# The last image's output products placed ahead of its attention sums, and the range check among the last results

## The chip, the cores and the metric

The kernel runs on one core of one Trainium2 chip. The metric is the device time of one execution in microseconds; the median of three runs before the change is 3424.28 us (3424.08 to 3426.5).

## What is computed

The reference has two layers on eight images of 64 x 64 positions with 256 channels. Layer 0 projects to q and k (v is k), does softmax attention in horizontal windows with half of the channels and in vertical windows with the other half, adds a depthwise 3 x 3 convolution of a hard-swish of v, takes a hard-swish of the sum (the context) and projects it with `w_out`. Layer 1 is attention over all 4096 positions of an image with 32-wide f, g and h, and a residual:

```
s    = g @ f^T ;  beta = softmax(s)
v    = beta @ h
out  = gamma * (v @ kv + bv) + x        # x = context @ w_out + b_out
```

So every output element is a product of the context with `w_out` plus a product of the attention's result with `wv` (scaled by gamma and a spectral norm) plus a bias. The two products are added in PSUM, the accumulator memory of TensorE.

## The kernel before, in words

Everything is float32, with channels on the 128 partitions and positions along the free axis, in blocks of TB = 512 positions. An image is a row of units: eight horizontal windows (h), eight vertical ones (v), and two global units (l), each of which handles half of the image's query positions (four blocks, one per quarter of 32 partitions) against all keys in 32 steps.

A step c of a global unit is: `scores` (four matmuls into two of three PSUM pairs s_0, s_1, s_2, L860), two exponentials on ACT (`weights_of`, L477), `weighted` (four matmuls into num_l, L876), and `add` on DVE (acc_l, L887), which sums the exponentials of all steps. The weighted product of a step is issued one step late (`flow.held`). When a unit's steps are over, these follow:

- `release` (L891) copies num_l to nums_l in SBUF on ACT.
- `sums` (L896) sums acc_l over partitions with four matmuls against ones; `copy_sums` (L497) copies the result to SBUF on ACT.
- `norm` (L902 on) takes the reciprocals on DVE (transpose L487, reciprocal L489, transpose L490) and multiplies nums_l with them (L904). In an image's second global unit it also calls `note` (L530), which keeps a running maximum and minimum of all reciprocals in the two tiles `seen`.
- `result(m, r)` makes the output: for output half m, r = 0 first issues four wv products (L915), one for each of the unit's four blocks, into two PSUM pairs with `start=True`; then, for two blocks at a time, 16 w_out products (`product`, L262) are added; then ACT adds the bias into an `ot` tile (L925) and SP issues its transfer to `out` (L926). There are two `ot` buffers (`out_bufs`).

The order of all engines' work is planned while the program is built. `Flow` keeps tasks in lanes with due times and estimated costs, and `flow.step` picks from them around each unit's scores; `flow.require(task)` issues a task and what it needs at once; `flow.drain` issues what is left. `result` tasks sit in the lane `res` and need `u.normed`. For all units but the last, there are score steps of the following unit to put around these tasks. For the last unit of the last image there is none: its sums, norm and results are issued by `flow.drain`, one behind the other.

PSUM is full with three s pairs (two banks each), num, and one bank (`mm_tile`) shared by all other products, the sums among them.

Behind the last image, the range check decides whether the fast way without subtracted maxima was valid. On DVE it takes the maximum and minimum of `seen` into `lim` (L1269, L1270), compares them with two limits (L1271, L1272), adds up the verdicts of all partitions with one matmul into `good` (L1274), and makes a flag (L1276, L1278). `nc.values_load` (L1279) loads the flag into a register of every engine, SP also asserts its bounds, and each engine branches (L1280) over an exact second pass, which does not run with these inputs. The tiles of the check come from a pool that is opened only then.

Of the kernel before, what the change touches and what calls it, by code (L numbers as in the profile page):

```python
# [5 lines left out]

# [6 lines left out]
F32 = mybir.dt.float32  # L13
I32 = mybir.dt.int32
AF = mybir.ActivationFunctionType
ALU = mybir.AluOpType
AX = mybir.AxisListType

P = 128
# [3 lines left out]
TB = 512  # L23
NB = N // TB
D = 32
NQ = P // D
L2_EPS = 1e-12

SUM_MAX, SUM_MIN = 1e20, 1e-20


def quad(r):
    return slice(r * D, (r + 1) * D)
# [225 lines left out]
def product(nc, out, lhsT, rhs, start=True, stop=True):  # L259

    for r in range(lhsT.shape[1] // D):
        nc.tensor.matmul(out[quad(r), :], lhsT=lhsT[:, quad(r)], rhs=rhs, start=start, stop=stop)  # L262
# [3 lines left out]
def tile_attention_blocks(  # L266
# [18 lines left out]
    nc = tc.nc  # L285
# [6 lines left out]
    def mm_tile(name):  # L292
        return ps_mm.tile([P, TB], F32, tag="mm", name=name)
# [4 lines left out]
    ones = const.tile([P, P], F32, name="ones")  # L298
# [29 lines left out]
    wout_sb = const.tile([P, 2, C], F32, name="wout_sb")  # L328
# [14 lines left out]
    wv_sb = const.tile([P, C], F32, name="wv_sb")  # L343
    bias_o = const.tile([P, 2], F32, name="bias_o")
# [58 lines left out]
    seen = [const.tile([P, 2 * NB + 2, TB // D], F32, name=f"seen{i}") for i in range(2)]  # L403
    for t in seen:
        nc.gpsimd.memset(t, 1.0)

    def attention(images, load_x, out_rows, exact):


# [2 lines left out]
        out_bufs = 1 if exact else 2  # L412
        state = pools.enter_context(tc.tile_pool(name=f"state{sfx}", bufs=1))
        xpool = pools.enter_context(tc.tile_pool(name=f"xpool{sfx}", bufs=2))
        work = pools.enter_context(tc.tile_pool(name=f"work{sfx}", bufs=2))
# [4 lines left out]
        ps_sc = pools.enter_context(tc.tile_pool(name=f"ps_sc{sfx}", bufs=1, space=PSUM))  # L420
# [7 lines left out]
        h_sb = state.tile([P, N // P, D], F32, name="h_sb")  # L428


        pairs = cycle([ps_sc.tile([P, 2, TB], F32, name=f"s_{i}") for i in range(3)])

        def combined_weights():

# [31 lines left out]
            return act[i // 2][:, k, start + cols.start : start + cols.stop]  # L466

        def sc_tiles():
            return [next(pairs), next(pairs)]

        def row_of(sc, r):
            return sc[r // 2][:, r % 2, :]
# [46 lines left out]
        def image(b):  # L519
# [311 lines left out]
            def global_unit(z):  # L831
                nm = f"{b}_l{z}"
                u = {}
# [74 lines left out]
                def result(m, r):  # L908
# [14 lines left out]
                    for q, j, po in blocks:  # L923
                        ot = work.tile([P, TB], F32, tag="ot", name=f"ot_{nm}_{q}_{m}", bufs=out_bufs)
                        nc.scalar.activation(ot, po, AF.Identity, bias=bias_o[:, m : m + 1])  # L925
                        nc.sync.dma_start(out=out_rows(b, m)[:, j * TB : (j + 1) * TB], in_=ot)  # L926

                return SimpleNamespace(
                    steps=4 * NB, scores=scores, weighted=weighted, add=add,
                    release=release, sums=sums, norm=norm, result=result,  # L930
                )

            return SimpleNamespace(
# [2 lines left out]
                project_fg=project_fg, fetch_fg=fetch_fg, project_h=project_h, turn_h=turn_h,  # L936
                h=[window_unit(0, i) for i in range(NB)],
                v=[window_unit(1, i) for i in range(NB)], l=[global_unit(z) for z in range(2)],
            )

        flow = Flow()
# [8 lines left out]
        units, t = [], 0  # L950
# [27 lines left out]
        def in_turn(tag, task):  # L978

            task.after += last_users[tag][-1:]  # L980

        def weights_ready(t):
            task = Task([])
            task.done, task.step = True, t
            weights[t] = task
            return task

        weights = {}
        for u in units:
            if not u.kind:  # L990
                continue
            e = u.t + u.steps
            w = [weights_ready(u.t + c) for c in range(u.steps)]
            if u.kind == "l":
                chain = None
                for c in range(1, u.steps):
                    task = flow.add(
                        "dve", [(partial(u.add, c), [("dve", ADD)])], u.t + c + DUE["add"],
                        [w[c]] + ([w[0]] if c == 1 else [chain]), ready=u.t + c + 1,
                    )  # L1000
                    if c == 1:
                        in_turn("acc", task)
                        readers[u.t].append(task)
                    readers[u.t + c].append(task)
                    chain = task
                total = flow.add(
                    "pe", [(u.sums, [("pe", PROD), ("act", COPY)])], e + 1, [chain], ready=e, bank=True
                )
                in_turn("sum", total)
                last_users["acc"].append(total)  # L1010
            else:
                acc = flow.add(
                    "dve", [(partial(u.add, 1), [("dve", ADD)])], u.t + 2, w[:2], ready=u.t + 2
                )
                in_turn("acc", acc)
                terms, pair = 3, acc
                if DUE["adds_v" if u.kind == "v" else "adds_h"]:
                    terms, acc = 2, flow.add(
                        "dve", [(partial(u.add, 2), [("dve", ADD)])], u.t + DUE["add2"],
                        [acc, w[2]], ready=u.t + 3,  # L1020
                    )
                pieces = [(partial(u.sums, n), [("pe", PROD / HALVES)]) for n in range(terms * HALVES)]
                pieces[-1] = (pieces[-1][0], [("pe", PROD / HALVES), ("act", COPY)])
                total = flow.add("pe", pieces, e, [acc, *w[2:]], ready=e, bank=True)
                total.then = (terms - 1, e + DUE["sums"])
                in_turn("sum", total)
                last_users["acc"].append(total)
                for c, task in enumerate(
                    (pair, pair, (total, 2) if terms == 3 else acc, (total, 1))
                ):  # L1030
                    readers[u.t + c].append(task)
            u.released = flow.add("act", [(u.release, [("act", COPY)])], e + DUE["release"], ready=e)
            shuffle = [("sp", ISSUE), ("dma", VIA)] if u.kind == "v" else []
            u.normed = flow.add(
                "dve", [(u.norm, [("dve", NORM), *shuffle])], e + DUE["norm"], [total, u.released], ready=e
            )
            last_users["sum"].append(u.normed)
            u.fetched = u.normed
            if u.kind == "v":
                u.fetched = flow.add("sp", [(u.fetch, [("sp", 4 * ISSUE), ("dma", FETCH)])], e, [u.normed])  # L1040
# [32 lines left out]
        for n, im in enumerate(ims):  # L1073
# [4 lines left out]
            for i in range(NB):  # L1078
                u = h[i]
# [4 lines left out]
                start = last.l[0].t if last else 0  # L1084
# [26 lines left out]
                for half in range(2):  # L1111
# [14 lines left out]
                    if p >= 0:  # L1126
                        k = 2 * p
# [58 lines left out]
            for z, u in enumerate(l):  # L1186
                u.ends = []
                for m in range(2):
                    pieces = [
                        (  # L1190
                            partial(u.result, m, r),
                            [("pe", 4 * PROD + (SCORES + DRAIN if r == 0 else 0)), ("act", 2 * EVICT)],
                        )
                        for r in (0, 2)
                    ]
                    u.ends.append(flow.add("res", pieces, u.t + u.steps + 4 * m, [u.normed], im.ends[-1:]))
                    im.ends.append(u.ends[-1])
                for r in range(NQ):
                    im.results[z * NQ + r] = u.ends
# [13 lines left out]
        for k, u in enumerate(units):  # L1213
            if u.kind:
                tag = ("ctxh", CTX) if u.kind == "h" else ("nums", 2)
# [32 lines left out]
        with tc.manual_schedule():  # L1248
            last = None
            for u in units:  # L1250
                for c in range(u.steps):
                    flow.step(partial(unit_scores, u, c), partial(unit_values, u, c, last))
                last = u
            flow.drain()
        pools.close()

    xv = xT.rearrange("b (k p) n -> b p k n", p=P)
    ov = out.rearrange("(b m p) n -> b m p n", m=2, p=P)
    attention(
        range(B),  # L1260
        lambda b, i: xv[b, :, :, i * TB : (i + 1) * TB],
        lambda b, m: ov[b, m],
        exact=False,
    )


    check = ctx.enter_context(tc.tile_pool(name="check", bufs=1))
    lim = check.tile([P, 2], F32, name="lim")
    nc.vector.tensor_reduce(lim[:, 0:1], seen[0], AX.XY, ALU.max)  # L1269
    nc.vector.tensor_reduce(lim[:, 1:2], seen[1], AX.XY, ALU.min)  # L1270
    nc.vector.tensor_single_scalar(lim[:, 0:1], lim[:, 0:1], SUM_MAX, ALU.is_le)  # L1271
    nc.vector.tensor_single_scalar(lim[:, 1:2], lim[:, 1:2], SUM_MIN, ALU.is_ge)  # L1272
    good = mm_tile("good")
    nc.tensor.matmul(good[0:1, 0:2], lhsT=ones[:, 0:1], rhs=lim, start=True, stop=True)  # L1274
    total = check.tile([1, 1], F32, name="total")
    nc.vector.tensor_reduce(total, good[0:1, 0:2], AX.X, ALU.add)  # L1276
    flag = check.tile([1, 1], I32, name="flag")
    nc.vector.tensor_copy(flag, total)  # L1278
    fine = nc.values_load(flag[0:1, 0:1], min_val=0, max_val=2 * P)  # L1279
    with tc.If(fine < 2 * P):  # L1280
        with tc.For_i(0, B) as b:
# [6 lines left out]
                exact=True,  # L1288
# [46 lines left out]
```

## Time and profile before

| | us |
|---|---|
| median of three runs | 3424.28 |
| the profiled execution's own time | 3424.36 |
| its span, first to last instruction | 3422.6 |
| PE (TensorE) busy in the span | 3334.3 |
| DVE (VectorE) busy | 2860.2 |
| ACT (ScalarE) busy | 2665.0 |
| last add of acc_l ends | 3389.26 |
| last w_out product ends | 3412.83 |
| flag written | 3414.55 |

Times in the trace are counted from the span's start. PEld is TensorE's weight load, which overlaps its matmuls. A float32 matmul of the program stands as two rows in the trace, so a block of 16 w_out products shows as x32. SPq, ACTq and so on are an engine's sequencer, which issues transfers, waits on semaphores and branches; these do not count as busy time. PEclk is the share of its full clock that TensorE was granted.

### The profile page before, as it was taken

The numbers are of one execution on the slowest core, as the hardware profiler recorded it, in microseconds if no ns is written. First come the engines' busy times: TensorE is split into PE (matmuls) and PEld (weight loads), VectorE is DVE, ScalarE is ACT, GpSimd is POOL, SyncE is SP. The second block draws the span as 40 slices with busy tenths as digits, with TensorE's granted clock in tenths as the row PEclk, the third lists the DMA queues.
The fourth block names the chain that finished last, engine by engine and source line by source line (L and its number), as shares of the span: only waits on it lengthen the run. The fifth ranks groups of instructions, "written<-read, shape, count | busy, mean of one in ns | idle before, by whom it ended". The sixth has DMA issues, their size and how long they took to land.

```text
span 3422.6 us, 78296 instructions
## 1 busy us (share of the span) xinstructions
PE 3334.3 (97%) x33780; PEld 1126.0 (33%) x33780; DVE 2860.2 (84%) x2340; ACT 2665.0 (78%) x3235; POOL 63.5 (2%) x266
## 2 busy tenths in 40 slices
PE   7989999999999999999999999999999999999997
PEld 3323333333333333333333333333333333333322
DVE  4778789887898879988799887998879988898876
ACT  5777787887878877788787887788877888778875
POOL 0000000000000000000000000000000000000000
PEclk9999999999999999999999999999999999999999
DMA  2122102221032210332112311123111231122200
GB/s 71 51 78 70 46 26 91 79 74 44 20 99 84 61 57 25 92 88 59 44 44 78 96 45 50 50 72 97 50 38 57 78 88 47 38 69 62 78 29 27
DMA packets 249411, 209.84 MB, mean 61 GB/s; under 512 B 26080, under 2 KB 190432, under 8 KB 249056
## 3 DMA queue, kind: packets, MB, share of 16 engines
q1 hardware_dynamic: 246816, 204.18, 20.2%
q8 instruction: 268, 4.39, 0.5%
q10 hardware_dynamic: 2240, 0.56, 0.1%
q14 instruction: 87, 0.71, 0.1%
HBM read 99.78 MB, written 83.89 MB: 54 GB/s over the span
## 4 chain that ended last, share of the span: by engine, by line
PE 70%; DVE 15%; ACT 8%; issue 4%; DMA 2%; SPq 1%; DVEq 0%; ACTq 0%
PE s L679 12%; DVE acc_l L887 11%; PE pq L262 11%; PE s L860 10%; PE num_l L876 9%; PE num_h L696 7%; PE s L262 6%; PE sum_h L714 5%; PE num_v L696 4%; ACT p_v L477 4%; PE sum_v L714 3%; DVE act L622 2%; PE pf L783 2%; ACT p_h L477 1%; PE s L915 1%
## 5 line engine op out<-in xcount | busy, mean ns | idle before, releaser
L887 DVE TENSOR_TENSOR acc_l<-acc_l,p_l 128x2048 f32<-128x2048 f32 x480 | 1099.6, 2291 | 224.3 <-ACT p_l L477 197.7
L477 ACT ACTIVATE p_l<-s 128x1024 f32<-128x1024 f32 x1024 | 991.4, 1023 | 188.4 <-PE s L860 121.6
L622 DVE SCALAR_TENSOR_TENSOR act<-hv,dw_sb,act 128x1024 f32<-128x1024 f32 x512 | 655.1, 1281 | 16.6 <-ACT act L618 2.3
L860 PE MATMUL s<-gq,f 32*128 32x512 f32 x4096 | 630.4, 640 | 3.8 <-ACT p_l L477 1.7
L477 ACT ACTIVATE p_h<-s 128x1024 f32<-128x1024 f32 x512 | 494.0, 1025 | 91.9 <-PE s L679 59.3
L477 ACT ACTIVATE p_v<-s 128x1024 f32<-128x1024 f32 x512 | 496.6, 1027 | 77.0 <-PE s L679 65.0
L876 PE MATMUL num_l<-p_l,h_sb 128*32 128x512 f32 x4096 | 546.4, 605 | 0.8 <-ACT nums_l L891 0.5
L262 PE MATMUL pq<-x,wqkv_sb 128*32 128x256 f32 x8192 | 520.5, 382 | 4.3 <-ACT qv L554 1.6
L262 PEld LDWEIGHTS pq<-x,wqkv_sb 128*32 128x32 f32 x8192 | 263.1, 110 | 361.4 <-issue 197.6
L679 PE MATMUL s<-qh,kh 32*128 32x512 f32 x2048 | 319.7, 640 | 11.4 <-ACT qh L551 6.6
L679 PE MATMUL s<-qv,kv 32*128 32x512 f32 x2048 | 327.3, 644 | 2.4 <-ACT p_v L477 2.4
L696 PE MATMUL num_v<-p_v,vs 128*32 128x512 f32 x2048 | 274.9, 609 | 21.2 <-DMA vs<-kvia 12.8
L860 PEld LDWEIGHTS s<-gq,f 32*128 32x128 f32 x4096 | 191.9, 183 | 311.8 <-issue 286.3
L696 PE MATMUL num_h<-p_h,vs 128*32 128x512 f32 x2048 | 272.8, 605 | 8.0 <-DMA vs<-kvia 3.3
L262 PE MATMUL s<-act,wout_sb 128*32 128x512 f32 x2048 | 227.4, 596 | 0.0
L925 ACT ACTIVATE ot_l<-s,bias_o 128x512 f32<-128x512 f32 x128 | 81.2, 684 | 179.8 <-PE s L262 168.5
L705 DVE TENSOR_TENSOR acc_v<-p_v,p_v 128x2048 f32<-128x2048 f32 x64 | 146.7, 2292 | 87.1 <-issue 60.5
L876 PEld LDWEIGHTS num_l<-p_l,h_sb 128*32 128x32 f32 x4096 | 80.7, 108 | 385.5 <-issue 370.7
L705 DVE TENSOR_TENSOR acc_h<-p_h,p_h 128x2048 f32<-128x2048 f32 x64 | 146.4, 2287 | 33.2 <-PE sum_v L714 15.6
L679 PEld LDWEIGHTS s<-qv,kv 32*128 32x128 f32 x2048 | 106.8, 184 | 181.3 <-issue 172.1
L679 PEld LDWEIGHTS s<-qh,kh 32*128 32x128 f32 x2048 | 94.0, 183 | 180.8 <-issue 140.3
L705 DVE TENSOR_TENSOR acc_v<-acc_v,p_v 128x2048 f32<-128x2048 f32 x64 | 146.2, 2284 | 4.8 <-ACT p_v L477 4.8
(126 smaller groups left out, 2464.4 us busy)
## 6 DMA issues: line engine op xcount, KB each, us to landing
x<-in_xT SPq DMA_DIRECT2D x92, 512.0 KB, 3.8
kvia<-kt SPq DMA_DIRECT2D x128, 256.0 KB, 2.5
vs<-kvia SPq DMA_DIRECT2D x512, 64.0 KB, 2.1
out<-ot_l SPq DMA_DIRECT2D x128, 256.0 KB, 2.1
via_v<-nums_v SPq DMA_DIRECT2D x64, 256.0 KB, 2.0
shuf_v<-via_v SPq DMA_DIRECT2D x256, 64.0 KB, 2.1
f<-fg SPq DMA_DIRECT2D x256, 64.0 KB, 2.0
gq<-fg SPq DMA_DIRECT2D x64, 64.0 KB, 2.0
```

Of the source, the lines that this page charges most:

```text
L262: nc.tensor.matmul(out[quad(r), :], lhsT=lhsT[:, quad(r)], rhs=rhs, start=start, stop=stop)
L477: nc.scalar.activation(pt[:, 2 * z : 2 * z + 2, :], sc[z], AF.Exp, scale=scale)
L622: nc.vector.scalar_tensor_tensor(o, src, wt, o, ALU.mult, ALU.add)
L679: nc.tensor.matmul(row_of(sc, r), lhsT=k[quad(r), c * P : (c + 1) * P], rhs=q[quad(r), :], start=True, stop=not exact,)
L696: nc.tensor.matmul(u["num"][quad(r), :], lhsT=vs[kind, i][:, r, c, :], rhs=u[c][:, r, :], start=(c == 0), stop=(c == 3),)
L705: nc.vector.tensor_add(u["acc"], u["acc"] if c == 2 else u[0], u[c])
L714: nc.tensor.matmul(u["sum"][quad(r), cols], lhsT=ones[:, :D], rhs=pt[:, r, cols], start=(k == 0), stop=(k == len(of) - 1),)
L783: nc.tensor.matmul(pf[quad(r), cols], lhsT=wcomb[:, k, quad(r % 2)], rhs=act_of(2 * p + r // 2, k, cols), start=(k == 0), stop=(k == 1),)
L860: nc.tensor.matmul(row_of(sc, r), lhsT=f4[quad(r), c * P : (c + 1) * P], rhs=gq[quad(r), z, :], start=True, stop=not exact,)
L876: nc.tensor.matmul(u["num"][quad(r), :], lhsT=h_sb[:, c, :], rhs=u[c][:, r, :], start=(c == 0), stop=(c == 4 * NB - 1),)
L887: nc.vector.tensor_add(u["acc"], u["acc"], u[c])
L925: nc.scalar.activation(ot, po, AF.Identity, bias=bias_o[:, m : m + 1])
```

## The change

For the last global unit of the last image in the fast pass, no `result` tasks are made. Two new functions issue its output in another order, written out by hand: `last_blocks(m, js)` issues the w_out products of output half m for two blocks into one PSUM pair (with `start` at the first and no stop), and `last_ends(m, js)` adds the wv products to them (`start=False, stop=True`) and issues the bias and the transfer. The PSUM pairs become a `deque`, so that one can be taken at a time.

The order at the end is now: w_out products of half 0, blocks 0 and 1; the last weighted product; w_out of half 0, blocks 2 and 3; sums and release; w_out of half 1, blocks 0 and 1; norm; wv and results of half 0; the range check's operations; wv and results of half 1, blocks 0 and 1; then w_out, wv and results of half 1, blocks 2 and 3.

The range check's pool is opened before the attention's, and its operations become the function `limits`, called between the results of half 0 and half 1. Loading the flag and the branch stay where they were in the source. In the built program, each engine's load of the flag is still the last thing before its branch, except on SP, where it stands behind the second of the last eight result transfers.

```diff
+    def limits():
+        nc.vector.tensor_reduce(lim[:, 0:1], seen[0], AX.XY, ALU.max)
+        nc.vector.tensor_reduce(lim[:, 1:2], seen[1], AX.XY, ALU.min)
+        nc.vector.tensor_single_scalar(lim[:, 0:1], lim[:, 0:1], SUM_MAX, ALU.is_le)
+        nc.vector.tensor_single_scalar(lim[:, 1:2], lim[:, 1:2], SUM_MIN, ALU.is_ge)
+        good = mm_tile("good")
+        nc.tensor.matmul(good[0:1, 0:2], lhsT=ones[:, 0:1], rhs=lim, start=True, stop=True)
+        nc.vector.tensor_reduce(total, good[0:1, 0:2], AX.X, ALU.add)
+        nc.vector.tensor_copy(flag, total)
...
+                def last_blocks(m, js):
+                    rows = slice(m * P, (m + 1) * P)
+                    if js[0] == 0:
+                        u["po", m] = []
+                    pair = pairs.popleft()
+                    pairs.append(pair)
+                    for i, j in enumerate(js):
+                        u["po", m].append(pair[:, i, :])
+                        for k in range(2):
+                            product(
+                                nc, u["po", m][j], wout_sb[:, k, rows], act_of(z * NQ + j, k),
+                                k == 0, False,
+                            )
+
+                def last_ends(m, js):
+                    rows = slice(m * P, (m + 1) * P)
+                    for j in js:
+                        nc.tensor.matmul(
+                            u["po", m][j], lhsT=wv_sb[quad(j), rows], rhs=u["num_sb"][quad(j), :],
+                            start=False, stop=True,
+                        )
+                    for j in js:
+                        ot = work.tile([P, TB], F32, tag="ot", name=f"ot_{nm}_{j}_{m}", bufs=out_bufs)
+                        nc.scalar.activation(
+                            ot, u["po", m][j], AF.Identity, bias=bias_o[:, m : m + 1]
+                        )
+                        i = z * NQ + j
+                        nc.sync.dma_start(out=out_rows(b, m)[:, i * TB : (i + 1) * TB], in_=ot)
...
+                    if u is units[-1] and not exact:
+                        continue
                     u.ends.append(flow.add("res", pieces, u.t + u.steps + 4 * m, [u.normed], im.ends[-1:]))
...
+            if not exact:
+                u.last_blocks(0, (0, 1))
+                flow.held()
+                flow.held = None
+                flow.t += 1
+                u.last_blocks(0, (2, 3))
+                flow.require(u.total, u.released)
+                u.last_blocks(1, (0, 1))
+                flow.require(u.normed)
+                u.last_ends(0, range(NQ))
+                limits()
+                u.last_ends(1, (0, 1))
+                u.last_blocks(1, (2, 3))
+                u.last_ends(1, (2, 3))
             flow.drain()
```

More of the change, by code (lines that the diff above doesn't have):

```diff
@@ L2 @@
 from contextlib import ExitStack
-from itertools import cycle
 from functools import cache, partial
@@ L405, in tile_attention_blocks @@
         nc.gpsimd.memset(t, 1.0)
+    check = ctx.enter_context(tc.tile_pool(name="check", bufs=1))
+    lim = check.tile([P, 2], F32, name="lim")
+    total = check.tile([1, 1], F32, name="total")
+    flag = check.tile([1, 1], I32, name="flag")
+    def limits():
[7 more added lines that the diff above has]
+        nc.vector.tensor_copy(flag, total)
     def attention(images, load_x, out_rows, exact):
@@ L428, in attention @@
         h_sb = state.tile([P, N // P, D], F32, name="h_sb")
-        pairs = cycle([ps_sc.tile([P, 2, TB], F32, name=f"s_{i}") for i in range(3)])
+        pairs = deque(ps_sc.tile([P, 2, TB], F32, name=f"s_{i}") for i in range(3))
         def combined_weights():
@@ L468, in sc_tiles @@
         def sc_tiles():
-            return [next(pairs), next(pairs)]
+            taken = [pairs.popleft(), pairs.popleft()]
+            pairs.extend(taken)
+            return taken
         def row_of(sc, r):
@@ L930, in global_unit @@
                     release=release, sums=sums, norm=norm, result=result,
+                    last_blocks=last_blocks, last_ends=last_ends,
                 )
@@ L1033, in attention @@
             shuffle = [("sp", ISSUE), ("dma", VIA)] if u.kind == "v" else []
+            u.total = total
             u.normed = flow.add(
@@ L1264, in tile_attention_blocks @@
     )
[L1267 to L1278, printed above, removed]
     fine = nc.values_load(flag[0:1, 0:1], min_val=0, max_val=2 * P)
```

## The prediction

> **What bounds the kernel now.** I read the page first, then the chain of waits, the timeline and the clock of the last 40 us, because the change touches only what follows the last image's last score step.
>
> ```profile
> span 3422.6 us, 78296 instructions
> PE 3334.3 (97%) x33780; PEld 1126.0 (33%) x33780; DVE 2860.2 (84%) x2340; ACT 2665.0 (78%) x3235; POOL 63.5 (2%) x266
> ```
>
> PE carries the kernel as a whole, but the tail is a different stage. The chain of waits (start, length, what), cut to its last part:
>
> ```profile
> 3386.96 2.30 DVE acc_l L887
> ...
> 3389.40 1.97 PE sum_l L896 x8
> 3391.39 0.59 ACT sum_sb_l L497
> ...
> 3394.53 2.09 PE s L915 x8
> 3396.62 8.09 PE s L262 x64
> 3404.71 1.07 PE s L915 x8
> 3405.78 7.05 PE s L262 x64
> 3412.85 0.45 DVE lim L1269
> ...
> 3414.41 0.14 DVE flag L1278
> ```
>
> The sums wait for DVE's last add (3389.26), the wv products wait for the norm (3394.49), and only then 15.1 us of w_out products start, which need neither. PE idles 4.2 us and 3.2 us on the way. The windows view gives the granted clock behind the DVE, ACT and POOL columns:
>
> ```profile
> 3383.00:3388.50 5.50, 1.97 (x8) 0.29 (x8) 5.29 (x3) 1.68 (x3) 0.00 (x0) 1.00 0.01 1
> 3388.50:3398.80 10.30, 6.20 (x28) 1.34 (x32) 3.85 (x7) 0.58 (x1) 0.00 (x0) 0.50 0.01 2
> ```
>
> After the idle stretch the clock is half for 10 us; that is why the sums take 1.97 us where num_l, four matmuls of the same shape, takes 1.07. What comes behind the flag the chain does not show; the views of L1279 and L1280, and SP's waits, do:
>
> ```profile
> L1279 SPq TENSOR_LOAD <-flag x1: 750/750/750, 3415.0 to 3415.0; - x1
> L1279 SPq SEQ_ASSERT  x1: 33/33/33, 3416.3 to 3416.3; - x1
> L1280 SPq COMPARE_BRANCH x1: 50/50/50, 3416.4 to 3416.4; - x1
> SPq L1280 <- SPq L1280: 4.2, 1, 4.2
> ```
>
> SP loads the flag, asserts its bounds, branches over the exact pass at 3416.4, and then stands 4.2 us before the next instruction. From there 1.9 us of semaphores and drains lead to 3422.6. So the end is: last result, flag, load, branch, fixed tail.
>
> **What the Trainium skill says.** "TensorE: Matmul & The Clock Gate", Part 1: an idle window of about 3.4 us drops the array to half rate until a busy one has passed. The trace agrees: 1.00, then 0.50 from 3388.5 to 3398.8. "DMA: Bandwidth & Descriptors", Anatomy of one DMA: about 2 us of fixed completion time per transfer; here 2.0 us at least and 2.1 in the middle for a 256 KB result. "Runtime: NRT & Kernel Launch", Instruction fetch mechanics: a taken branch outside the prefetched pages stalls on a fetch; the 4.2 us fit that, though only the stall, not its cause, is in the trace.
>
> **The change part by part.** The instruction order of the built program is unchanged on every queue up to the last score step. Behind it nothing is added: the same 64 w_out, 8 wv, 4 sum and 1 check matmul of the tail and the same eight result transfers, in another order. I replay that order with this trace's durations. A block of 16 w_out matmuls is half of a warm L262 row: 7.05/2 = 3.53 us.
>
> *PE.* num_l of step 30 ends at 3382.96. Block m0/q01 to 3386.49; num_l of step 31 (+1.07) to 3387.56; block m0/q23 to 3391.09. The banks are free: the exponentials that read them ended by 3384.1. The sums now start at 3391.09 instead of 3389.40, so they are 1.7 us late, but PE has not idled, so I take the warm 1.07: 3392.16, 0.8 us later than before. Block m1/q01 runs to 3395.69.
>
> *Norm.* From the sums' end to the product's end it took 3394.49 - 3391.37 = 3.12 us; now 3395.28. The nums copy, now behind the sums' copy on ACT (0.58 us), lies beside DVE's two transposes and reciprocal (1.7 us): nothing. PE is still on m1/q01, so the norm is hidden, and wv for m0 (1.07 warm) ends at 3396.76, its first half at 3396.23.
>
> *Range check.* The two seen updates end 0.74 after the norm, 3396.02; the four lim operations took 1.02 (3397.04). The good matmul, in PE's queue behind wv m0, waits some 0.4 us for lim, ends near 3397.4; the flag is ready at 3397.7. The 1.7 us of check work after the last w_out (3412.83 to 3414.55) leave the end.
>
> *PE's rest.* wv m1/q01 (0.53) to 3397.9, block m1/q23 to 3401.5, its wv to 3402.0. Before, PE ended at 3412.83: 10.8 us earlier. But PE then no longer sets the end.
>
> *ACT and the result buffers.* There are two ot buffers. Each result must have landed before its buffer is written again; before, PE gave pairs only every 3.4 to 4.6 us, which hid this. Where it shows today, in ACT's timeline of the image's first half and in the view of the ot_l tile:
>
> ```profile
> 3329.47 0.69 ACT L925 ACTIVATE ot_l<-s,bias_o 128x512 f32<-128x512 f32 x1 [2.22 <-PE s L262]
> 3331.35 0.69 ACT L925 ACTIVATE ot_l<-s,bias_o 128x512 f32<-128x512 f32 x1 [1.19 <-DMA out<-ot_l]
> DMA to landing us min/median/max: 2.0/2.1/4.4
> ```
>
> A buffer's round is 0.71 (ACT start to SP issue: 3401.36 to 3402.07) + 2.1 + 0.08 = 2.9 us. The first pair starts at 3396.30; three rounds later, 3405.0, starts the last pair (1.27 us for two): 3406.27 against 3414.17 before. PE's last block is ready at 3402.0, 3 us ahead.
>
> *SP.* Its flag load now sits between the second and third result transfer, with six transfers queued behind it. SP is free at 3397.9; semaphores 0.42, then 1.35 from load to assert: 3399.8, just when the third result (3399.2 + 0.7) is ready. I charge 0.1 us. Behind the last transfer (3406.3 + 0.33) only the branch is left: 3406.7 against 3416.44, **9.7 us earlier**. The 4.2 us fetch I keep; with the other engines branching at other times it may be 3.4 (ACT's, 3415.66 to 3419.07) or, beside two transfers in flight, up to 1.4 longer (estimate: those transfers' own time). The last landing, 3408.4, is under it. ACT, last of the other engines, loads its own flag after the last result (0.82), branches near 3407.2 and is back by 3410.6, just ahead of SP's 3410.9.
>
> Sum: 7.9 us from the results, 1.9 from check and load leaving the end, less 0.1. The profiled execution took 3424.36 (span 3422.6 and 1.8 around it), 0.1 above the median of 3424.28. Forecast: 3424.3 - 9.7 = **3414.6 us**.
>
> **The rivals.**
> *Longer rounds or fetch.* One transfer at 4.0 us, as at 3327.3 (issue to landing), adds 1.9; a fetch slowed by the last transfers adds 1.4. For it: ACT waited for a landing four times, 11.3 us in all, earlier in this run. Against: at the tail no loads share the queues, and its eight landings took 2.0 to 2.3. Gain 6.4 to 8.3: 3416 to 3418.
> *The clock falls anyway.* If PE is at half rate from 3388.55 to 3398.79 as now: block m0/q23 ends at 3393.6, sums 3395.6, m1/q01 3400.7, first pair 5 us later. Gain 4.7: 3419.6. Against: the longest gap that I find is 0.4 us.
> *Not as written.* A scheduler could hold the w_out blocks behind the norm, and the gain would be the check's 1.9 us alone: 3422.4. The built order speaks against it.
> *Slower than before.* The check's tiles are now allocated ahead of the attention's pools, so every later on-chip tile sits at a shifted address. If this slows the 480 acc_l adds (1099.6 us busy, 11% of the chain, 376 us), the gain is cancelled at 9.7/376 = 2.6% on each (2291 to 2350 ns); at 5% the kernel ends 9 us slower: 3433. Nothing shows that addresses matter here, and shapes are the same.
>
> **How the numbers follow.** A measurement of this kernel can tell about 0.2%, 6.8 us, so faster means below 3417.4. Forecast as worked out, 3412.5 to 3416: 0.74. Longer rounds or fetch: 0.15, of which 0.03 fall above 3417.4. Half clock: 0.05, within 0.2%. Not as written: 0.02, within. Slower: 0.04. That is 0.86 faster, 0.10 the same, 0.04 slower. The range starts where fetch (-0.8) and rounds (3 x -0.1) are best and the runs' spread of 2.4 us is taken by half, 3412.2, and ends with the longer rounds, 3418.3.
>
> **What would show it.** In the profile after: the clock 1.00 through 3383 to 3402; sums at 1.07 us; no PE gap over 1 us before wv; ACT's ot rows paced 2.9 us with DMA as releaser; the flag cast near 3397.7; SP's branch near 3406.7 and its stall of 4.2; the adds still 2291 ns. A half clock, a third transfer issued well after 3399.9, rounds above 3.3 us, a stall over 6 us, or longer adds would each prove its step wrong.

## The result, and the profile after

The changed kernel takes 3417.38 us in the median (3415.27 to 3420.03, 11 runs) against 3424.55 (3422.58 to 3426.85, 11 runs): 7.2 us less, ratio 0.9979 with a 95% interval of 0.997 to 0.9988. Measured once more, the same two kernels gave 3417.62 and 3424.8, ratio 0.9976 (0.9968 to 0.9984). Both intervals leave out no change; the size is just beyond the 0.2% that the prediction took as the least that can be told here. The profiled execution took 3416.28, so the two profiled executions are 8.1 us apart. From here on every time is from the profile that the text names.

The page's head, and the windows view over the new tail (columns as before; the clock is the third number from the end):

```profile
span 3414.5 us, 78286 instructions
PE 3331.6 (98%) x33780; PEld 1126.4 (33%) x33780; DVE 2860.6 (84%) x2340; ACT 2668.8 (78%) x3235; POOL 63.5 (2%) x266
```

```profile
3383.00:3402.60 19.60, 19.09 (x166) 5.46 (x158) 10.55 (x15) 5.36 (x9) 0.00 (x0) 1.00 0.15 56
```

PE is busy for 19.1 of 19.6 us at the full clock, where before it idled for 7.4 us in two gaps and had the half clock for 10 us. The chain of waits, last part:

```profile
3383.16 3.43 PE s L261 x32
...
3390.89 0.86 PE sum_l L913 x8
3391.75 3.43 PE s L261 x32
3395.18 1.08 PE s L963 x8
...
3396.29 0.70 ACT ot_l L969
...
3397.00 2.04 DMA out<-ot_l
...
3400.50 3.70 DMA out<-ot_l
...
3404.28 0.70 ACT ot_l L969
...
3404.99 2.60 DMA out<-ot_l
...
3407.67 0.69 ACT ot_l L969
```

The wait for DVE's last add, the norm and the range check have left the chain; the sums stand in it only as work of PE between two blocks. In their place stand three landings of result transfers, each followed by the ACT instruction that had to wait for its buffer. ACT's timeline says the same, with the releaser at the end of each row:

```profile
3396.29 1.27 ACT L969 ACTIVATE ot_l<-s,bias_o 128x512 f32<-128x512 f32 x2 [3.39 <-PE s L963]
3399.14 1.33 ACT L969 ACTIVATE ot_l<-s,bias_o 128x512 f32<-128x512 f32 x2 [1.59 <-DMA out<-ot_l]
3402.22 0.69 ACT L969 ACTIVATE ot_l<-s,bias_o 128x512 f32<-128x512 f32 x1 [1.75 <-DMA out<-ot_l]
3404.28 1.46 ACT L969 ACTIVATE ot_l<-s,bias_o 128x512 f32<-128x512 f32 x2 [1.37 <-DMA out<-ot_l]
3407.67 0.69 ACT L969 ACTIVATE ot_l<-s,bias_o 128x512 f32<-128x512 f32 x1 [1.94 <-DMA out<-ot_l]
```

The first round is 2.85 us (3396.29 to 3399.14), forecast 2.9; the two that start next take 3.1 and 4.5 (3399.14 to 3402.22, 3399.78 to 3404.28). The last result ends at 3408.36, forecast 3406.27. The views of the flag, of the branch line and of SP's waits complete the end:

```profile
L420 DVE CAST flag<-total x1: 141/141/141, 3397.2 to 3397.2; 1x1 int32<-1x1 f32 x1
```

```profile
L1334 POOLq COMPARE_BRANCH  x1: 45/45/45, 3398.3 to 3398.3; - x1
L1334 DVEq COMPARE_BRANCH  x1: 72/72/72, 3398.5 to 3398.5; - x1
L1334 PEldq COMPARE_BRANCH  x1: 4032/4032/4032, 3400.1 to 3400.1; - x1
L1334 SPq COMPARE_BRANCH  x1: 50/50/50, 3409.1 to 3409.1; - x1
```

```profile
SPq L1334 <- SPq L1334: 3.5, 1, 3.5
```

Two things are new here. SP branches at 3409.1, 7.4 us earlier than before, and its stall is 3.5 instead of 4.2. And DVE and PE load the early flag and branch at 3398.5 and 3400.1, in the middle of the result transfers. DVE's work is over by then; PE's sequencer branches while PE's last matmuls run on to 3402.6. POOL branches at 3398.3. In the DMA view of 3400.5 to 3404.2, the stretch of the transfer that took 3.70 us to land, queues 8 and 14 carry instructions:

```profile
q1 hardware_dynamic: 369, 0.69, 49.7%
q8 instruction: 1, 0.02, 1.5%
q14 instruction: 1, 0.01, 0.9%
```

That suggested theory A: the rounds of the two result buffers set the end, and the instruction fetches of engines that now branch early lengthen the landings in these rounds. Rival B: the landings are slow of themselves, two transfers at a time. Rival C: something else sets the end, PE's rest or SP's flag load.

### The profile page after: what moved, and what is told of

Read it like the earlier page. It is cut to its first block, busy times and chain, and to the rows that moved or that the text cites. A ratio compares the mean times of both kernels' runs of the same rounds, so it can differ in the third digit from the quotient of the medians.

```text
span 3414.5 us, 78286 instructions
## 1 busy us (share of the span) xinstructions
PE 3331.6 (98%) x33780; PEld 1126.4 (33%) x33780; DVE 2860.6 (84%) x2340; ACT 2668.8 (78%) x3235; POOL 63.5 (2%) x266
## 4 chain that ended last, share of the span: by engine, by line
PE 71%; DVE 14%; ACT 8%; issue 4%; DMA 2%; SPq 1%; DVEq 0%; ACTq 0%
PE s L696 12%; PE s L877 11%; PE pq L261 11%; DVE acc_l L904 10%; PE num_l L893 10%; PE num_h L713 7%; PE s L261 6%; PE sum_h L731 5%; PE num_v L713 4%; ACT p_v L494 4%; PE sum_v L731 3%; DVE act L639 2%; PE pf L800 2%; ACT p_h L494 1%; PE s L932 1%
## 5 line engine op out<-in xcount | busy, mean ns | idle before, releaser
L904 DVE TENSOR_TENSOR acc_l<-acc_l,p_l 128x2048 f32<-128x2048 f32 x480 | 1099.8, 2291 | 224.5 <-ACT p_l L494 197.9
```

The costliest lines, as they stand in the source:

```text
L904: nc.vector.tensor_add(u["acc"], u["acc"], u[c])
```

## The experiments

All edits are against the changed kernel unless the text says otherwise. Each ratio is to the kernel before on the same chip; the first four shared one chip (before: 3423.15 us), the last three another (3424.8 us). Each experiment has one profile. The place in the span where the tail begins varies from profile to profile by some us (DVE's last add ends between 3385.6 and 3389.8), so I compare stretches inside the tail: from the start of the first result on ACT to the end of the last.

### Eight result buffers

```diff
-ot = work.tile([P, TB], F32, tag="ot", name=f"ot_{nm}_{j}_{m}", bufs=out_bufs)
+ot = work.tile([P, TB], F32, tag=("qh", "kh")[m], name=f"ot_{nm}_{j}_{m}", bufs=QH)
```

> The changed kernel, with the last unit's eight results in eight buffers of their own (the idle ones of qh and kh) instead of two in turn. Theory A (rounds of the two result buffers set the end, and their landings are lengthened by instruction fetches of engines that branch early): ACT no longer waits for a landing, the last result follows PE's last product (3402.6) and ends near 3403.9 instead of 3408.4, SP branches near 3404.4 instead of 3409.1; 4 to 5 us faster than the changed kernel, 11 to 13 us faster than before. Rival B (rounds set the end, but slow landings come from the transfers themselves, which stand two at a time): the same here, landings above 2.3 stay. Rival C (PE's rest or SP's flag load sets the end): no change, 0 to 1 us.

Measured: 3411.35 us, ratio 0.9968 (0.9956 to 0.998), 11.8 us under before. ACT's timeline:

```profile
3394.30 3.58 ACT L969 ACTIVATE ot_l<-s,bias_o 128x512 f32<-128x512 f32 x6 [3.40 <-PE s L963]
3400.70 1.26 ACT L969 ACTIVATE ot_l<-s,bias_o 128x512 f32<-128x512 f32 x2 [2.82 <-PE s L963]
```

No row waits for a DMA any more. Six results run back to back, the last two follow PE, and first to last takes 7.66 us (3394.30 to 3401.96) against 12.07 in the changed kernel: 4.4 us less. SP branches at 3402.7. So the buffers' rounds did set the end, and rival C falls. The landings themselves became longer (up to 3.6 us, with up to four transfers in flight and instruction packets beside the longest; this run does not separate the two), which no longer matters. Theory A and rival B both expected this result; the next experiment tells them apart.

### The branches of DVE and PE held back

```diff
+hold = check.tile([P, 2], F32, name="hold")
+nc.vector.tensor_copy(hold, u.last_ot[:, 0:2])
+held = mm_tile("held")
+nc.tensor.matmul(held[0:1, 0:2], lhsT=ones[:, 0:1], rhs=hold, start=True, stop=True)
```

Here `u.last_ot` is the buffer of the last result.

> The changed kernel, with one small DVE copy out of the last result and one small matmul of it added behind everything, so that DVE and PE branch after the last result, while the flag stays early for SP. Theory A (fetches of early branches lengthen the landings): all landings that ACT waits for are 2.0 to 2.3 us, the last result ends near 3406.3 instead of 3408.4; the end itself gains less, 0 to 2 us, since PE and DVE then fetch last. Rival B (landings are slow of themselves): landings of 2.3 to 3.7 us again, last result near 3408, and the kernel slower than the changed one by 0 to 1 us.

Measured: 3414.88 us, ratio 0.9975 (0.9965 to 0.9984), 8.3 us under before. ACT's timeline:

```profile
3395.72 1.27 ACT L970 ACTIVATE ot_l<-s,bias_o 128x512 f32<-128x512 f32 x2 [3.40 <-PE s L964]
3398.57 1.33 ACT L970 ACTIVATE ot_l<-s,bias_o 128x512 f32<-128x512 f32 x2 [1.58 <-DMA out<-ot_l]
3401.42 1.33 ACT L970 ACTIVATE ot_l<-s,bias_o 128x512 f32<-128x512 f32 x2 [1.53 <-DMA out<-ot_l]
3404.27 1.33 ACT L970 ACTIVATE ot_l<-s,bias_o 128x512 f32<-128x512 f32 x2 [1.51 <-DMA out<-ot_l]
```

The rows start 2.85 us apart, every time. The six landings that are waited for took 2.02 to 2.11 us, and first to last is 9.88 us; the prediction's sum gave 9.97 for this stretch. In the DMA view of the same stretch as above (from the issue of the fourth transfer, 3.7 us long) no instruction packet starts:

```profile
q1 hardware_dynamic: 406, 0.77, 54.8%
```

Nothing about these transfers was changed, only when DVE and PE branch. So rival B falls: the 2.2 us of excess in the changed kernel come with the early branches of DVE and PE. That the branches act through their fetches is read from the packets (see the last section). POOL still branches early here, and one 8 KB instruction packet starts at 3399.22, beside a landing of 2.04, which it did not lengthen. The end itself gains less: from the first result to the span's end it is 16.4 us, against 18.2 and 17.7 in the two profiles of the changed kernel (the second is below), because PE is now the last to come back:

```profile
L1342 POOLq COMPARE_BRANCH  x1: 45/45/45, 3397.7 to 3397.7; - x1
L1342 SPq COMPARE_BRANCH  x1: 50/50/50, 3406.3 to 3406.3; - x1
L1342 PEldq COMPARE_BRANCH  x1: 3662/3662/3662, 3407.3 to 3407.3; - x1
```

Whether it beats the changed kernel the intervals can't tell.

### The range check late

```diff
-                limits()
...
+    limits()
     fine = nc.values_load(flag[0:1, 0:1], min_val=0, max_val=2 * P)
```

> The changed kernel, with the range check's operations called behind the last results, as before, but with its tiles still allocated first. DVE and PE then load the flag and branch only after PE's last product, near 3403 to 3404, not near 3398 and 3400. Theory A: the landings of the first two pairs of results go back to 2.0 to 2.3 us, the last result ends near 3406.3 to 3407.0; SP's flag load is in time for the last pair, so the kernel is 1 to 2 us faster than the changed one. Rival B: landings and time as in the changed kernel, or up to 1.5 us slower for the later flag.

Measured: 3414.56 us, ratio 0.9973 (0.9962 to 0.9983), 8.6 us under before. The branches of DVE and PE, and ACT's timeline:

```profile
L1334 PEldq COMPARE_BRANCH  x1: 4212/4212/4212, 3402.3 to 3402.3; - x1
L1334 DVEq COMPARE_BRANCH  x1: 72/72/72, 3402.6 to 3402.6; - x1
```

```profile
3394.99 1.26 ACT L969 ACTIVATE ot_l<-s,bias_o 128x512 f32<-128x512 f32 x2 [3.40 <-PE s L963]
3397.84 1.32 ACT L969 ACTIVATE ot_l<-s,bias_o 128x512 f32<-128x512 f32 x2 [1.58 <-DMA out<-ot_l]
3400.72 1.31 ACT L969 ACTIVATE ot_l<-s,bias_o 128x512 f32<-128x512 f32 x2 [1.55 <-DMA out<-ot_l]
3403.56 0.69 ACT L969 ACTIVATE ot_l<-s,bias_o 128x512 f32<-128x512 f32 x1 [1.54 <-DMA out<-ot_l]
3404.78 0.69 ACT L969 ACTIVATE ot_l<-s,bias_o 128x512 f32<-128x512 f32 x1 [0.53 <-DMA out<-ot_l]
```

DVE and PE branch at 3402.6 and 3402.3, 7.6 and 7.3 us after the first result's start (in the changed kernel 2.2 and 3.8). The first four landings took 2.03 to 2.11 us; of the two that the last pair waits for, one took 2.65. First to last is 10.48 us: between the other two, as theory A says. SP's flag load fits ahead of the last pair and costs nothing. SP's stall was 4.4 us, though, so from the first result to the span's end it is 17.6 us, against 18.2 and 17.7 in the two profiles of the changed kernel. The 1 to 2 us expected over the changed kernel can't be told. So for this order the late check is no worse than the early one, as far as the intervals show: the order of the w_out products gives the gain without the check's move.

### Only the check moved early, order of before

The kernel before, with the check's pool opened first and `limits` called after the results of half 0; no `last_blocks`, no `last_ends`:

```diff
                         nc.sync.dma_start(out=out_rows(b, m)[:, j * TB : (j + 1) * TB], in_=ot)
+                    if not exact and b == B - 1 and z and (m, r) == (0, 2):
+                        limits()
```

> The kernel before, with only the range check moved: its operations between the results of half 0 and half 1, its tiles allocated first. The w_out and wv order is that of before. By the prediction's steps: the last result ends as before (3414.2), and the 1.9 us of check, flag load and assert leave the end: SP branches near 3414.6 instead of 3416.4, 1.6 to 2.6 us faster than before (the upper end if SP's fetch is as short as in the changed kernel, 3.5 instead of 4.2). If the check was hidden anyway: 0.

Measured: 3422.06 us, ratio 0.9996 (0.9988 to 1.0004): 1.1 us under before, less than the 1.6 to 2.6 expected. The interval neither tells it from no change nor rules the expectation out (0.9988 is 4.1 us). The step itself is there: from the last result's end to SP's branch it was 2.27 us (3414.17 to 3416.44) and is 0.70 (3415.15 to 3415.84), 1.6 us less. Part of it goes to PE's clock in the profile. The half-clock stretch lies 1.9 us later here. That shortens the sums by 0.5 us (1.45 against 1.94), and the 64 rows of half 0's w_out products that meet it take 0.95 us longer:

```profile
3396.56 9.11 PE L261 MATMUL s<-act,wout_sb 128*32 128x512 f32 x64
3405.49 0.19 PE L418 MATMUL good<-lim,ones 128*1 128x2 f32 x2
```

The same row before:

```profile
3396.55 8.16 PE L262 MATMUL s<-act,wout_sb 128*32 128x512 f32 x64
```

SP's stall is 0.5 us shorter (3.7 against 4.2), and from DVE's last add to the span's end it is 31.8 us against 33.3. So the check's move is worth about 1.6 us in the order of before, where PE sets the end. In the new order, where the result buffers set it, the late check showed no loss against the early one. The larger part of the gain is the order of w_out.

### The changed kernel again

> The changed kernel once more, as it is, on the chip of the two runs that follow. Theory A (landings lengthened where an instruction fetch is in flight, by branches that come early): among the landings that ACT waits for, those with a fetch beside them are above 2.2 us, those without are 2.0 to 2.2; the last result ends 10 us after the first one starts plus the excess of these landings over 2.1; 6 to 9 us faster than before. Rival B (slow landings of themselves): long landings without a fetch beside them.

Measured: 3417.62 us, ratio 0.9976 (0.9968 to 0.9984). First to last 11.69 us. The six landings waited for: 2.03, 2.12, 2.40, 3.69, 2.00 and 2.24. The DMA view shows one packet on each instruction queue beside the 3.69 again, and one on q8 beside the 2.00, so a fetch in flight does not always lengthen a landing, which I had expected of it; but of these six none above 2.2 stands without one.

### The first two blocks behind the sums

```diff
-                u.last_blocks(0, (0, 1))
                 flow.held()
                 flow.held = None
                 flow.t += 1
-                u.last_blocks(0, (2, 3))
                 flow.require(u.total, u.released)
+                u.last_blocks(0, (0, 1))
+                u.last_blocks(0, (2, 3))
                 u.last_blocks(1, (0, 1))
```

> The changed kernel, with its first two blocks of w_out products put behind the sums instead of ahead of and between the last weighted product and the sums; all else as changed. By the prediction's clock step, PE idles again from 3385 to 3389.4, and the half clock comes back for about 7 to 10 us: sums in 1.5 to 2 us, first results near 3405 instead of 3396.3, last result near 3415 to 3417, no faster than before: -1 to +2 us. If the clock played no part and only the order counted: the three blocks (10.6 us) from 3390.5, first results near 3402, last near 3412, 3 to 5 us faster than before.

Measured: 3423.04 us, ratio 0.9997 (0.9988 to 1.0005): the whole gain is gone. PE's timeline and the windows view:

```profile
3385.94 1.91 PE L913 MATMUL sum_l<-acc_l,ones 128*32 128x512 f32 x8 [4.20 <-DVE acc_l L904]
3387.54 11.46 PE L261 MATMUL s<-act,wout_sb 128*32 128x512 f32 x96
```

```profile
3386.00:3389.50 3.50, 3.50 (x20) 1.18 (x24) 0.96 (x2) 1.07 (x2) 0.00 (x0) 0.51 0.02 5
3389.50:3402.00 12.50, 12.32 (x113) 4.13 (x107) 3.34 (x11) 1.27 (x2) 0.00 (x0) 1.00 0.03 10
```

The 4.2 us gap is back, and with it the half clock, but for 3.4 us only, not for the 7 to 10 that I expected. In the kernel before it lasted 10.2 us, and there PE idled again behind the sums, while here it had work without a gap; that this made the difference is argued from the two traces, not tested. At full rate these 3.4 us of work take half, 1.7 us. From the end of DVE's last add to the first result it is 14.3 us (3385.79 to 3400.11); in the changed kernel 6.8 (3389.46 to 3396.29), 7.5 less. The two blocks that now stand behind the sums are 6.9 of it (3.43 each), the clock 1.7, less 1.1 by which the sums here start sooner after the add. So most of the gain is cover, not clock: 5.8 us net from work put into time in which PE would wait for DVE, and about 1.7 us of clock on top in this profile.

### Eight buffers, and the last bias on DVE

On top of the eight buffers:

```diff
+if (m, j) == (1, NQ - 1):
+    nc.vector.tensor_scalar_add(ot, u["po", m][j], bias_o[:, m : m + 1])
+else:
     nc.scalar.activation(ot, u["po", m][j], AF.Identity, bias=bias_o[:, m : m + 1])
```

> The eight buffers of the first experiment, and the very last result's bias added by DVE beside ACT instead of behind it. Theory A: as the eight buffers, with the last result 0.5 us earlier: 11 to 13 us faster than before; the DVE now branches behind it, so that fewer fetches fall beside the transfers. Rival: DVE's later branch becomes the last to come back and sets the end; then the same as eight buffers or 0.5 us slower.

Measured: 3412.04 us, ratio 0.9962 (0.9948 to 0.9976), 12.8 us under before and the largest gain here, though its interval overlaps that of the eight buffers alone. DVE's last row:

```profile
3399.52 0.75 DVE L970 TENSOR_SCALAR ot_l<-s,bias_o 128x512 f32<-128x512 f32 x1 [6.09 <-ACT ot_l L972]
```

DVE took the last result's bias at 3399.52, 0.72 after ACT's began, because the addition, by the waits of the profile, was released by ACT's instruction and not by PE, so nothing was gained by working side by side; first to last is 7.86 us, against 7.66. The 0.5 us that I expected did not come. DVE, which branches at 3400.9 and is back at 3404.4, does not set the end (SP is back at 3404.6).

## Why the prediction was right

It said 3414.6, range 3412.2 to 3418.3, faster with 0.86; the median is 3417.38, inside the range, with the gain 7.2 of 9.7 us. The median lies where the prediction put its rival of longer rounds (3416 to 3418, chance 0.15), above the 3412.5 to 3416 of its main case (0.74). It is also only 0.02 us below the 3417.4 that the prediction drew as the limit of faster, and the interval of the ratio reaches to both sides of that limit: that it fell on this side is luck.

- **PE order and clock: right.** Forecast sums at 3391.1 and warm, PE never idle for over 1 us; measured 3390.7, 1.04 us, and one gap of 0.51 us, at the check's matmul.
- **First result at 3396.30: right (3396.29), by two errors that cancel.** On the chain a block of w_out took 3.43 us, not 3.53, and num_l and the sums 0.86 each, not 1.07, so wv started 0.6 us earlier than summed; but ACT's first result waited for all four wv products, not for the first two.
- **Range check: right.** Flag at 3397.3 (forecast 3397.7), third transfer issued at 3399.86 (forecast just behind 3399.8, where the sum's own terms give 3399.7), so SP's early flag load costs nearly nothing.
- **Rounds of the result buffers: the mechanism right, the size off.** I put 2.1 us for every landing; 2.26 and 3.70 were measured in the second round, 2.00 and 2.60 in the third. The stretch is 12.07 us instead of 9.97: 2.1 us lost. I had this as a rival (one transfer at 4.0), but looked for its cause in loads that share the queues, and argued that none are there. The cause was the change itself: an early flag lets DVE and PE branch early, and their fetches meet the transfers. I asked what transfers in flight do to a fetch, but not what a fetch does to them. I followed the flag load on SP's queue and what was queued behind it, and did not follow it on DVE's and PE's, where nothing waits. The trace of before had a hint: of the tail's eight landings, the two slowest (2.25 and 2.29) have a 16 KB instruction packet beside them. The section that I cited for 2 us of fixed time describes transfers that GpSimd issues and counts the data's own time on top; here, where SP issues them, an undisturbed landing of 256 KB took 2.0 to 2.3 us with its data.
- **SP's end: two small terms.** From the last issue to the branch it took 0.34 us where I had 0.07; the stall was 3.5 us instead of 4.2, which I had named as possible. Together 0.4 us better than the forecast.

Sum against the profile: 9.7 - 2.1 - 0.3 + 0.7 = 8.0; measured 8.1. The median's gain of 7.2 is one more us lower; the runs of both kernels spread over 4 us, and the profiles show tails that begin up to 4 us apart, so I name no cause for it.

The other rivals: the clock did not fall (it does when the blocks are taken away again); the acc_l adds measured 2291 ns as before, so shifted addresses cost nothing there.

## What to carry to other kernels

When work is moved off the end of a kernel, look at what the wait it leaves behind used to hide: here result buffers that were in time at 3.5 us a pair became the bound at 2.9, and idle buffers of other tiles, taken for the last results, gave 4 us more than the reordering. A branch or a flag that comes early on an engine with nothing left to do is not free: here it made transfers that do count land up to 1.6 us later. Work that does not need what an engine waits for belongs ahead of the wait, not behind it, even where the wait itself ends later by it (here the sums started 1.3 us later and the first result came 5 us sooner).

## What the runs showed of the hardware

A result transfer lands in sixteen parts. In the changed kernel's trace I counted for each of the 128 result transfers whether an instruction packet (queue 8 or 14) was in flight between issue and landing. The 82 without one landed in 2.0 to 2.3 us. The 46 with one took 2.7 in the median and up to 4.4, though 13 of them landed within 2.3. The kernel before has the same split (88 at 2.0 to 2.2, 40 up to 4.4), so in this kernel the long landings are all among those with an instruction packet beside them. By itself that is no proof, since a longer landing also has more time to meet a packet; the experiment with the branches held adds that the long landings of the tail go when the branches come later.

In the 3.70 us case fifteen parts had landed by 2.11, and one came 1.6 us behind. Its packets show more. From 3402.2 to 3403.7 the only data packets are eight of 2 KB, one sixteenth of the transfer. The first starts at 3402.62, where the 16 KB packet of queue 8 (3401.74 to 3402.64) ends, and they run one behind another to 3403.70. In the second profile of the changed kernel, beside the 3.69, the first of eight such packets starts at 3402.93 and the 16 KB packet ends at 3402.94. So both times one sixteenth of the data started only as an instruction packet ended. That the two were on the same DMA engine is argued from these times; the trace doesn't name the engine.
